# A two-layer graph network: one aggregate's products split a second time by Strassen in panel 3 of layer 0

## The chip, the cores and the metric

The kernel runs on one core of one Trainium2 chip. The time is the device time of one execution in microseconds (us); the number given for a kernel is the median of its runs. A profile records one further execution. In its views PE is the matmul engine, PEld its weight loads, DVE the vector engine, ACT the scalar engine, POOL the GpSimd engine and SP the engine that issues most DMAs; "L678" is line 678 of the kernel.

## What is computed

Two graph layers on 2708 nodes with 1024 features. Both normalise the rows, apply a relu, form attention scores between all nodes, mask them with the adjacency, take a softmax over the columns and multiply the attention by a projected matrix; the input is added back.

```python
h = jnp.maximum(_layernorm(x, axis=-1), 0.0)          # layer 0
f = h @ Wf + bf;  g = h @ Wg + bg
e = jax.nn.relu(f @ g.T)
attention = jax.nn.softmax(jnp.where(adj > 0, e, NEG), axis=1)
x = x + attention @ (h @ W + bW)

h = jnp.maximum(_layernorm(x, axis=-1), 0.0)          # layer 1
hw = h @ W1
e = jax.nn.leaky_relu(hw @ a1 + (hw @ a2).T, negative_slope=0.2)
attention = jax.nn.softmax(jnp.where(adj > 0, e, NEG), axis=1)
x = x + jax.nn.relu(attention @ hw)
```

Everything is fp32. The kernel uses that attention @ (h @ W) is (attention @ h) @ W: it first makes the *aggregate* attention @ h, then projects it.

## The kernel before

**Panels and pairs.** The 2708 rows are 20 tiles of 128 rows, one further tile and a rest of 20 rows (tiles 20 and 21, called MONO and TINY). The output rows are worked on in five panels of 576, 576, 532, 512 and 512 rows. The 20 full tiles form NQ = 10 pairs q = (2q, 2q+1), and two pairs form one of NK = 5 groups k.

**One level of Strassen.** Each large product is split once in Strassen's way (Winograd's form): seven products M1, M5, M2, M6, M3, M7, M4 in place of eight, with sums of the left and right operands in front of them and sums of the results behind. In the aggregate the left operand is h (split by halves of the features and by the even or odd tile of a pair), and the right operand is the transposed attention of a panel (split by the even or odd tile and by halves `lo`, `hi` of the panel's columns). A product of a 512-row panel is ten k-steps of four matmuls 128x128 by 128x256.

**Left operands in DRAM.** Layer 0's seven left operands lie in `hg_d[i]`, one DRAM tensor for each group i, with rows of W = 512 values. `rows_h` stores the four that are plain blocks of h (M1, M5's part, M2, M4), and `sums_h` makes the three sums in place. Layer 1's lie in `hr_d`, written by `pair_h`.

**The plain aggregate.** `aggregate(l, p, S, sm, then, rate)` (L923) makes the right sums on DVE (`second`, `fourth`) and calls `accumulate` (L664), which emits the matmuls of a product (L678) and after some k-steps and at the end of a product calls `behind(rate)`, four times a product. A left block for layer 0 is a load of 512 KB (`hc`, one group of one product), issued by `load` when its first matmul is emitted. `left_over` adds MONO and TINY to three results, `into_m15` to the fourth. PSUM results are evicted by DVE and ACT into `gT`; POOL scales them by the inverse row sums (L1020).

**The aggregate split twice.** `aggregate_quartered` (L1086) serves panels 1 to 4 of layer 1. Each of the seven products is split again: `product(m, n, ps, start)` (L1099) emits one of seven inner products, five groups k by two matmuls of (128x128 by 128x128 when the panel has 512 rows), L1113. The right inner sums are made on DVE by `make(m)` from `quarters_of` (L1033), 20 subtractions a product, into `quarter` tiles. The left inner sums of layer 1 are made earlier by `put_quarters(m, k)` (L405): a load of 512 KB in two halves issued by POOL into `hq`, four adds or subtractions of 256 columns on DVE, two stores of 256 KB by POOL into `hs2_d`. An inner product loads its left blocks (`hc2`, four groups, from `hr_d` or `hs2_d`), and a product loads the blocks of the fifth group once (`hl2`, two loads). `V` holds the product until it is added into its places.

**The order of the work.** For each panel p of layer 0: scores(p), project_q(p+1), aggregate(0, p), project(0, p). In front of the panel 4 aggregate stand scores(4) and project(0, 3). Two queues of small work are fed in between matmuls by a planner with prices in us: `later` (softmax pieces at 1.4, rows of the next layer, and so on) and `lazy` (the left sums of layer 1 at 1.7 each). `behind(us)` adds to a credit, and pops pieces while credit is left; `lazy` is served only when `later` is empty and `spare[0]` is set, which is so in layer 0's aggregates of panels 1 to 4. A piece's loads are issued ahead of it, when it is near the head of the list (`one`):

```python
def behind(us, psum_free=False):
    credit[0] = min(credit[0] + us, 2 * us)
    while later and credit[0] > 0 and ...:
        credit[0] -= one()
    while spare[0] and not later and lazy and credit[0] > 0:
        credit[0] -= one(lazy)
```

`softmax(p)` puts 24 pieces at the head of `later`. It is called after M2 of project_q, which from then on calls `behind(1.5)` 20 times; an aggregate calls `behind(3.0)` 28 times. Layer 1's seven left sums of a panel p enter `lazy` during scores(p+1), so that each of the aggregates of panels 1, 2 and 3 serves seven.

**What fixes an order.** `load` (L136) issues on SP and keeps program order. `store` (L140) issues on POOL, without it. `held(f)` keeps the vector instructions that f emits behind the vector instruction emitted before each; `by_gpsimd` (L1669) does the same for a DMA on POOL. Otherwise the scheduler at compile time may move an instruction. All stream tiles (`hc`, `hq`, `hc2`, `hl`, `hl2`, `adj_i`, `md`, ...) come from one pool of 12 tiles of 4 KB a partition; `slot` tiles come from a pool of 54.

Of the kernel before, what the change touches and what calls it, by code (L numbers as in the profile page):

```python
# [57 lines left out]
def kernel(  # L58
# [95 lines left out]
    groups = [[q, q + 1] for q in range(0, NQ, 2)]  # L154
    group_of = {q: (i, j) for i, g in enumerate(groups) for j, q in enumerate(g)}
    assert sorted(group_of) == list(range(NQ))
    hg_d = [dram.tile([P, 7, len(g), W], FP, name=f"hg_d{i}") for i, g in enumerate(groups)]
    NK = NQ // 2
    WH = W // 2
    hr_d = dram.tile([P, 7, 2, 2, NK, WH], FP, name="hr_d")  # L160
    hs2_d = dram.tile([P, 7, 4, NK, WH], FP, name="hs2_d")

# [41 lines left out]
    def one(of=None):  # L204
        of = later if of is None else of
        for it in of[:4 if of is lazy and from_slots[0] else ahead[0]]:
            if it[1]:
                it[1]()
                it[1] = None
        us, _, go = of.pop(0)[:3]  # L210
        go()
        return us
# [155 lines left out]
    def rows_h(q, ha, hb):  # L368

        i, j = group_of[q]  # L370
        for m, h in ((M1, ha[0]), (M5, ha[1]), (M2, hb[0]), (M4, hb[1])):
            store(hg_d[i][:, m, j], h)
# [3 lines left out]
    def sums_h():  # L376

        def fetch(q, two):
            i, j = group_of[q]
            for m in (M1, M2):  # L380
                two.append(stream("hr", (P, 2, W)))
                (load if "m" in got else by_scalar)(two[-1], hg_d[i][:, m:m + 2, j])

        def first(q, two):
            (a0, a1), (b0, b1) = ((t[:, 0], t[:, 1]) for t in two)
            add(b1, a1, b1)
            sub(a1, a0, a1)

        def second(q, two):
            (a0, a1), (b0, b1) = ((t[:, 0], t[:, 1]) for t in two)  # L390
            sub(a0, b1, a0)
            sub(b0, b0, a0)
            i, j = group_of[q]
            store(hg_d[i][:, M6:M7 + 1, j], two[0])
            store(hg_d[i][:, M3, j], b0)
            store(hg_d[i][:, M5, j], b1)
            summed[0] += 1
        for q in range(NQ):
            two = []
            put(1.4, lambda q=q, two=two: held(first, q, two), lambda q=q, two=two: fetch(q, two), ready=lambda: sums_may[0])  # L400
            put(1.4, lambda q=q, two=two: held(second, q, two), ready=lambda: sums_may[0])

    BY_QUARTERS = (M1, M5, M2, M6, M7, M3, M4)
    made_quarters = {}

    def put_quarters(m, k, to=lazy):
# [3 lines left out]
        def fetch():  # L410
            if from_slots[0]:
                two.extend(slot(f"hq{h}", (P, 2, WH)) for h in range(2))
            else:
                t = stream("hq", (P, 4, WH))
                two.extend(t[:, 2 * h:2 * h + 2] for h in range(2))
# [3 lines left out]
        def go():  # L419
# [5 lines left out]
            for h in range(2):  # L425
                store(hs2_d[:, m, 2 * h:2 * h + 2, k], two[h])
            made_quarters[m] = made_quarters.get(m, 0) + 1
        put(1.7, go, fetch, to=to)

    def quarters_until(m):  # L430
        while made_quarters.get(m, 0) < NK:
# [491 lines left out]
    def aggregate(l, p, S, sm, then={}, rate=3.0):  # L923
# [29 lines left out]
        steps = [(m, i) for m in order_of_products for i in range(len(groups))]  # L953

        def left(m, q, d):
            i, j = group_of[q]
            at = steps.index((m, i))
            for m_, i_ in steps[at:at + (3 if l else 1)]:
                if (m_, i_) not in hc:
                    hc[m_, i_] = stream("hc", (P, 4, WH) if l else (P, 2, W))  # L960
                    load(hc[m_, i_], hr_d[:, m_, :, :, i_].rearrange("p h f c -> p (h f) c") if l else hg_d[i_][:, m_])
# [71 lines left out]
    def quarters_of(p, S):  # L1033
# [50 lines left out]
        return {"make": make, "right": right, "first": first, "fifth": fifth, "second": second, "fourth": fourth}  # L1084

    def aggregate_quartered(p, S, sm, of_right, then={}, fine=1.2):  # L1086
# [12 lines left out]
        def product(m, n, ps, start):  # L1099
            quarters_until(m)  # L1100
            if (m, 0) not in lasts:
                for i, of in enumerate((hr_d[:, m, :, :, NK - 1].rearrange("p h f c -> p (h f) c"), hs2_d[:, m, :, NK - 1])):
                    lasts[m, i] = stream("hl2", (P, 4, WH))
                    load(lasts[m, i], of)
# [3 lines left out]
            load(t, hr_d[:, m, i // 2, i % 2, :NK - 1] if raw else hs2_d[:, m, i, :NK - 1])  # L1108
# [11 lines left out]
        def left_over(banks, e, s, fresh):  # L1120

            two = stream("hl", (P, W + 2 * P))
            load(two, hgl_d[1][:, e])
# [44 lines left out]
        def with_second():  # L1168
# [4 lines left out]
                       M7: lambda: make(M3), M3: lambda: make(M4)}  # L1173
        left_out = None
        for m in BY_QUARTERS:
            V = [quad(*direct[m])[:, 2 * r:2 * r + 2] for r in range(2)] if m in direct else [v[:, :, :h] for v in in_pairs("V")]
# [40 lines left out]
            if m == M5:  # L1217
                of_right["second"]()
            if m == M5:
                inverse.append(inverse_sums(p, sm))  # L1220
# [357 lines left out]
    def rows_done(t, xt):  # L1578
# [14 lines left out]
        if panel_of[t] == NP - 1:  # L1593
# [18 lines left out]
            else:  # L1612
# [16 lines left out]
                if q == NQ - 1:  # L1629
                    for m in BY_QUARTERS:  # L1630
                        put_quarters(m, q // 2, later)
# [17 lines left out]
        elif whole:  # L1649
# [3 lines left out]
            if quads_met[q // 2] == 2:  # L1653
                put(0.0, lambda: [put_quarters(m, q // 2) for m in BY_QUARTERS])
# [12 lines left out]
    ORDERED = (NP - 1,)  # L1667

# [98 lines left out]
    for p in range(NP):  # L1767
# [21 lines left out]
        G[p] = aggregate(0, p, S, got["sm"], then)  # L1789
        spare[0] = False  # L1790
        if p == 0:
            flush()
# [114 lines left out]
    for p in range(NP):  # L1907
# [6 lines left out]
        g = aggregate_quartered(p, S, sm, next_right, then, fine=1.0) if p else aggregate(1, p, S, sm, then, rate=4.0)  # L1914
# [34 lines left out]
```

## Time and profile before

| | us |
|---|---|
| median of 3 runs (lowest, highest) | 3050.46 (3048.57, 3051.97) |
| the profiled execution, its own time | 3055.39 |
| its span in the profile | 3053.6 |
| PE busy in the span | 2999.1 |
| DVE busy in the span | 2048.9 |
| layer 0, aggregate of panel 1 (from 839.95 to 988.06) | 148.11 |
| layer 0, aggregate of panel 2 (from 1236.95 to 1374.00) | 137.05 |
| layer 0, aggregate of panel 3 (from 1611.16 to 1743.16) | 132.00 |

All durations that follow come from the profiled execution; its span is 1.8 us shorter than its own time, and that time is 4.9 us above the median of the runs. In the profile's tables, "x" stands before a number of instructions. A wait is written "who <- whom it waited for: us in total, times, longest". Of the DMA, "share" is the mean busy share of the 16 DMA engines, and GB/s is what they moved. Times of instructions are counted from the start of the span.

### The profile page before, as it was taken

To read this page: it belongs to the slowest core of one execution; us is meant where nothing else is said; L and a number is where in the kernel's file an instruction comes from. 1 tells how busy PE (TensorE), PEld (TensorE's weight loads), DVE (VectorE), ACT (ScalarE), POOL (GpSimd) and SP (SyncE) were. 2 spreads that over 40 slices of the span, in tenths; PEclk is the share of its full clock that TensorE was granted. 3 is DMA by queue.
4 is the path that set the end of the run, shared out by engine and by line. 5 is a ranking of instruction groups with operands and counts; after the bars stand their busy time and mean duration, and the time that the engine had idled before them with its cause. 6 is when DMAs were issued, how large, how long until landed. Compare 5 with 4: busy or idle time off the path is not lost.

```text
span 3053.6 us, 41717 instructions
## 1 busy us (share of the span) xinstructions
PE 2999.1 (98%) x14642; PEld 2300.7 (75%) x14642; DVE 2048.9 (67%) x4667; ACT 536.5 (18%) x880; POOL 495.2 (16%) x770
## 2 busy tenths in 40 slices
PE   8998999999999999999999999999999999999999
PEld 4576777667877588885888886784767959879695
DVE  5776794585742686616965376867878768887863
ACT  3420020020200221101220111202232131212200
POOL 1421111210112110223101111131212010020201
PEclk9999999999999999999999999999999999999999
DMA  6989978887466785768957587678757768878797
GB/s 228 303 271 269 313 277 308 268 281 235 131 236 164 233 271 192 245 156 258 291 186 251 176 244 252 238 293 324 257 190 265 260 200 298 292 266 296 258 302 267
DMA packets 392704, 766.78 MB, mean 251 GB/s; under 512 B 65728, under 2 KB 206944, under 8 KB 392464
## 3 DMA queue, kind: packets, MB, share of 16 engines
q1 hardware_dynamic: 332336, 584.80, 59.4%
q0 software_dynamic: 54464, 164.78, 16.1%
q10 hardware_dynamic: 5696, 14.55, 1.4%
q8 instruction: 116, 1.90, 0.2%
q14 instruction: 92, 0.75, 0.1%
HBM read 630.04 MB, written 138.11 MB: 252 GB/s over the span
## 4 chain that ended last, share of the span: by engine, by line
PE 70%; issue 12%; DVE 11%; DMA 4%; POOL 2%; ACT 1%; SPq 0%; POOLq 0%; DVEq 0%; ACTq 0%
PE gy L678 6%; PE gz L678 6%; PE sz L1424 5%; PE gz L1113 5%; PE gx L678 5%; PE pz L1313 4%; PE px L1313 4%; PE sy L1424 3%; PE sx L1424 3%; PE gx L1113 3%; PE M_ps L591 3%; PE py L1313 3%; PE gy L1113 3%; PE gv L678 3%; DVE P L45 2%
## 5 line engine op out<-in xcount | busy, mean ns | idle before, releaser
L1424 PE MATMUL sz<-B,As 128*128 128x288 f32 (+2 forms) x1200 | 292.9, 393 | 5.4 <-DVE st L45 5.2
L1424 PEld LDWEIGHTS sz<-B,As 128*128 128x128 f32 x1200 | 228.3, 191 | 54.5 <-DVE st L45 8.4
L1424 PE MATMUL sx<-B,As 128*128 128x288 f32 (+2 forms) x800 | 201.3, 395 | 11.0 <-DMA As<-hs_d 9.3
L1424 PE MATMUL sy<-B,As 128*128 128x288 f32 (+2 forms) x800 | 199.0, 392 | 0.0
L1424 PEld LDWEIGHTS sx<-B,As 128*128 128x128 f32 x800 | 152.8, 192 | 44.0 <-DMA As<-hs_d 9.7
L678 PE MATMUL gz<-Sa,hc 128*128 128x288 f32 (+2 forms) x800 | 185.8, 393 | 0.0
L678 PEld LDWEIGHTS gz<-Sa,hc 128*128 128x128 f32 x800 | 151.7, 190 | 32.0 <-issue 2.2
L1424 PEld LDWEIGHTS sy<-B,As 128*128 128x128 f32 x800 | 152.0, 190 | 30.4 <-DVE st L45 0.3
L1113 PE MATMUL gz<-quarter,hc 128*128 128x128 f32 (+2 forms) x1344 | 168.9, 279 | 3.8 <-DVE gT L45 3.7
L1113 PEld LDWEIGHTS gz<-quarter,hc 128*128 128x128 f32 x1344 | 160.6, 191 | 5.1 <-DVE gT L45 4.6
L143 POOL DMA_DIRECT2D out_dram<-x_res x164 | 81.0, 500 | 469.1 <-DVE x_res L45 463.1
L1313 PE MATMUL py<-w,ps 128*128 128x512 f32 x320 | 142.1, 593 | 0.0
L1313 PE MATMUL pz<-w,ps 128*128 128x512 f32 x320 | 142.0, 595 | 0.0
L1313 PE MATMUL px<-w,gT 128*128 128x512 f32 x320 | 141.1, 593 | 0.0
L678 PE MATMUL gy<-T,hc 128*128 128x288 f32 (+2 forms) x480 | 115.0, 402 | 3.8 <-DMA hc<-hg_d 3.8
L1313 PEld LDWEIGHTS pz<-w,ps 128*128 128x128 f32 x320 | 60.3, 190 | 76.2 <-issue 72.1
L1313 PEld LDWEIGHTS py<-w,ps 128*128 128x128 f32 x320 | 60.6, 190 | 75.0 <-issue 72.6
L591 PE MATMUL M_ps<-wgT,wfT 128*128 128x512 f32 x256 | 112.7, 597 | 1.6 <-ACT hsT L45 1.6
L1313 PEld LDWEIGHTS px<-w,gT 128*128 128x128 f32 x320 | 60.2, 190 | 71.2 <-issue 67.8
L678 PEld LDWEIGHTS gy<-T,hc 128*128 128x128 f32 x480 | 93.2, 194 | 24.6 <-DMA hc<-hg_d 4.3
L143 POOL DMA_DIRECT2D mk_d<-mask x55 | 35.9, 652 | 455.6 <-DVE mask L45 427.3
L45 ACT ACTIVATE P<-P 128x576 f32<-128x576 f32 (+3 forms) x111 | 72.1, 650 | 207.3 <-DVE P L45 207.3
(391 smaller groups left out, 5829.0 us busy)
## 6 DMA issues: line engine op xcount, KB each, us to landing
hc<-hg_d SPq DMA_DIRECT2D x175, 512.0 KB
As<-hs_d SPq DMA_DIRECT2D x150, 512.0 KB
hc<-hr_d SPq DMA_DIRECT2D x119, 512.0 KB
hc<-hs_d SPq DMA_DIRECT2D x112, 512.0 KB
w<-wt_d SPq DMA_DIRECT2D x96, 512.0 KB
w<-in_L_gnn_W_dram SPq DMA_DIRECT2D x72, 512.0 KB
md<-md_d SPq DMA_DIRECT2D x56, 512.0 KB
adj_i<-in_adj_dram SPq DMA_DIRECT2D x200, 128.0 KB
```

Source lines behind the costliest of these rows:

```text
L45: i = f(*a, **k)
L143: nc.gpsimd.dma_start(a, b)
L591: nc.tensor.matmul(ps, wfT[a][c // NH][:, c % NH, :], wgT[b][c], start=(c == 0), stop=(c == NC - 1))
L678: nc.tensor.matmul(ps[d], left(m, k, d), right(m, k), start=(start and k == 0), stop=(k == K - 1), skip_group_check=True)
L1113: nc.tensor.matmul(ps[:, d], lhs[:, d * P:(d + 1) * P], inner_right(m, n, k), start=(start and k == 0 and d == 0), stop=(k == NK - 1), ski ...
L1313: nc.tensor.matmul(ps, left[i][m][:, k, :], w_[k], start=(start and k == 0), stop=(k == NH - 1), skip_group_check=True)
L1424: nc.tensor.matmul(ps[:n, :h], lefts[q][:, i % 2, c, :n], B[m][c // 2][:, c % 2, :h], start=(start and c == 0), stop=(c == NH - 1), skip_g ...
```

## The change

Layer 0's aggregate of panel 3 is made by `aggregate_quartered` too, with a new first argument l. In layer 0 its products M1 and M5 stay plain (through `accumulate`, rate 3.0), and M2, M6, M7, M3, M4 are split again, in this order; `behind` is called with 1.2 after each inner product. `V` takes a stream tile there. Their left inner sums are 25 new pieces of `lazy` (five products by five groups), put there after the aggregate of panel 0, at a price of 1.7. Each loads 512 KB from `hg_d` on SP in program order, does its four vector instructions held in order, and stores 2 x 256 KB by POOL in order into a second `hs2_d`. `lazy` now fetches for three pieces ahead instead of `ahead[0]`. `hg_d` becomes one tensor for all groups. An inner product of layer 0 that takes plain blocks loads them from `hg_d` in pieces of 1 KB.

```diff
-    hg_d = [dram.tile([P, 7, len(g), W], FP, name=f"hg_d{i}") for i, g in enumerate(groups)]
+    hg_d = dram.tile([P, 7, NK, 2, W], FP, name="hg_d")
-    hs2_d = dram.tile([P, 7, 4, NK, WH], FP, name="hs2_d")
+    hs2_d = [dram.tile([P, 7, 4, NK, WH], FP, name=f"hs2_d{l}") for l in range(2)]
...
     def one(of=None):
-        for it in of[:4 if of is lazy and from_slots[0] else ahead[0]]:
+        for it in of[:(4 if from_slots[0] else 3) if of is lazy else ahead[0]]:
...
-    BY_QUARTERS = (M1, M5, M2, M6, M7, M3, M4)
+    BY_QUARTERS = ((M2, M6, M7, M3, M4), (M1, M5, M2, M6, M7, M3, M4))
...
-    def put_quarters(m, k, to=lazy):
+    def put_quarters(l, m, k, to=lazy):
         def fetch():
+            if l == 0:
+                t = stream("hq", (P, 2, 2, WH))
+                load(t.rearrange("p f h c -> p f (h c)"), hg_d[:, m, k])
+                two.extend(t[:, :, h] for h in range(2))
+                return
...
             for h in range(2):
-                store(hs2_d[:, m, 2 * h:2 * h + 2, k], two[h])
-            made_quarters[m] = made_quarters.get(m, 0) + 1
-        put(1.7, go, fetch, to=to)
+                (by_gpsimd if l == 0 else store)(hs2_d[l][:, m, 2 * h:2 * h + 2, k], two[h])
+            made_quarters[l, m] = made_quarters.get((l, m), 0) + 1
+        put(1.7, (lambda: held(go)) if l == 0 else go, fetch, to=to)
...
-    def aggregate_quartered(p, S, sm, of_right, then={}, fine=1.2):
+    def aggregate_quartered(l, p, S, sm, of_right, then={}, fine=1.2, rate=3.0):
...
             if (m, 0) not in lasts:
-                for i, of in enumerate((hr_d[:, m, :, :, NK - 1].rearrange("p h f c -> p (h f) c"), hs2_d[:, m, :, NK - 1])):
+                rows = hr_d[:, m, :, :, NK - 1] if l else hg_d[:, m, NK - 1].rearrange("p f (h c) -> p h f c", h=2)
+                for i, of in enumerate((rows, hs2_d[l][:, m, :, NK - 1])):
                     lasts[m, i] = stream("hl2", (P, 4, WH))
-                    load(lasts[m, i], of)
+                    if l or i:
+                        load(lasts[m, i], of if i else of.rearrange("p h f c -> p (h f) c"))
+                    else:
+                        for h_ in range(2):
+                            load(lasts[m, i][:, 2 * h_:2 * h_ + 2], of[:, h_])
...
-            load(t, hr_d[:, m, i // 2, i % 2, :NK - 1] if raw else hs2_d[:, m, i, :NK - 1])
+            load(t, hs2_d[l][:, m, i, :NK - 1] if not raw else hr_d[:, m, i // 2, i % 2, :NK - 1] if l else
+                 hg_d[:, m, :NK - 1, i % 2, i // 2 * WH:(i // 2 + 1) * WH])
...
+        def collected():
+            if l == 0:
+                t = stream("V", (P, NH, h))
+                return [t[:, 2 * r:2 * r + 2, :h] for r in range(2)]
+            return [v[:, :, :h] for v in in_pairs("V")]
+
+        if l == 0:
...
+            exps_until(NQ)
+            of_right["fifth"]()
+            accumulate(left, of_right["operand"], NQ, h, (M1, M5), then,
+                       {M1: first_product, M5: lambda d, ps: add(quad(0, hi)[:, d], ps, quad(0, lo)[:, d])}, "g",
+                       {M5: sums_of_columns}, rate=rate, by_k=True, more={(M5, NQ // 2): with_second})
...
-        for m in BY_QUARTERS:
+        for m in BY_QUARTERS[l]:
...
+    SPLIT_EARLY = (3,)
...
-        G[p] = aggregate(0, p, S, got["sm"], then)
+        if p in SPLIT_EARLY:
+            G[p] = aggregate_quartered(0, p, S, got["sm"], quarters_of(p, S), then)
+        else:
+            G[p] = aggregate(0, p, S, got["sm"], then)
         spare[0] = False
         if p == 0:
+            for m in BY_QUARTERS[0]:
+                for k in range(NK):
+                    put_quarters(0, m, k)
             flush()
```

## The prediction

> **What bounds the kernel now.** I read the page first, then the busy time of each engine by stage, then the tensor engine's instructions in order of time, then waits, and last the DMA rate in stretches of 10 us around the panel 1 aggregate.
>
> The page's first part says that the matmul engine is the bound nearly everywhere:
>
> ```profile
> PE 2999.1 (98%) x14642; PEld 2300.7 (75%) x14642; DVE 2048.9 (67%) x4667; ACT 536.5 (18%) x880; POOL 495.2 (16%) x770
> ```
>
> By stage (stretch, its length, busy PE, weight loads, DVE, ACT, POOL, granted clock, DMA share, GB/s). The rows are layer 0's aggregates of panels 1, 2 and 3, then layer 1's of panels 3 and 4, which are already split twice:
>
> ```profile
> 839.95:988.06 148.11, 148.11 (x629) 114.35 (x629) 47.74 (x110) 6.04 (x13) 27.79 (x28) 1.00 0.66 200
> 1236.95:1374.00 137.05, 137.05 (x630) 114.34 (x629) 45.02 (x109) 4.60 (x11) 28.39 (x31) 1.00 0.69 208
> 1611.16:1743.16 132.00, 132.00 (x630) 114.35 (x629) 47.18 (x117) 11.13 (x16) 20.40 (x21) 1.00 0.71 223
> 2702.00:2830.00 128.00, 125.69 (x1132) 122.54 (x1131) 103.08 (x296) 23.06 (x44) 5.89 (x12) 1.00 0.87 301
> 2877.00:3000.00 123.00, 121.84 (x1115) 120.13 (x1114) 77.78 (x239) 8.71 (x20) 3.92 (x8) 1.00 0.90 304
> ```
>
> PE has no idle microsecond in the three aggregates of layer 0, so a microsecond that PE saves or waits there is one of the total. DVE has room (48 of 148). DMA is the second resource.
>
> The price of both forms of a product stands in PE's order of time (start, length, shape; two records are one matmul). Panel 3 as it is, then layer 1's panel 3:
>
> ```profile
> 1611.00 17.43 PE L678 MATMUL gx<-Sa,hc 128*128 128x256 f32 x80
> 1628.27 17.43 PE L678 MATMUL gy<-T,hc 128*128 128x256 f32 x80
> ...
> 2723.90 1.95 PE L1113 MATMUL gz<-quarter,hc 128*128 128x128 f32 x16
> 2725.68 0.61 PE L1113 MATMUL gz<-quarter,hl 128*128 128x128 f32 x4
> 2726.13 1.95 PE L1113 MATMUL gy<-quarter,hc 128*128 128x128 f32 x16
> ```
>
> A plain product takes 1628.27 - 1611.00 = 17.27 us (40 matmuls of 256 columns). An inner product takes 2726.13 - 2723.90 = 2.23 us (10 of 128), seven of them 15.63 us.
>
> **What the Trainium skill says.** "TensorE: Matmul & The Clock Gate", section "Back-to-back issue gap", gives N/2.4 + 2.5 ns for a matmul of N columns. The trace agrees up to a factor of four for this fp32 work: 17.27/40 = 432 ns is 4 x 108, 15.63/70 = 223 ns is 4 x 56. The saving is thus nearly the 1/8 of the columns, less the fixed part. "DMA: Bandwidth & Descriptors", section "Issuing engines are not separate DMA queues", says that DMAs started by SP, ACT and POOL run on the same 16 engines and interleave; its "Specifications" give a ceiling of 435 GB/s. Here the rate stops at 418 GB/s with share 1.03 (below), so moving a transfer to another queue makes no room. The first page's section "What's actually happening" says that an idle window of about 3.4 us halves the clock. The trace has that too, in layer 0's panel 0 aggregate, where DMA was full (chain in order of time: start, us):
>
> ```profile
> 506.16 7.68 DMA hc<-hg_d
> 513.88 7.18 PE gy L678 x16
> 521.07 19.40 PE gz L678 x80
> ```
>
> PE stood 7.7 us for its left blocks, then took 7.18 us for 16 records that take 19.40/5 = 3.88 warm: 3.3 us more.
>
> **Part 1: panel 3's matmuls.** Five products at 17.27 - 15.63 = 1.64 us less: -8.2. The left-over rows (tiles 20 and 21) cost four bursts, 2.46 us each in plain form (1659.35 to 1661.81) and 2.53 in the split form (2751.57 to 2754.10): +0.3. The order M1, M5, M2, M6, M7, M3, M4 swaps two products and costs nothing. Sum: **-7.9 us** of PE.
>
> **Part 2: panel 3's vector work.** Five times 20 subtractions for the right sums at 282 ns (row quarter<-P): 28 us. Evictions: 28 adds from PSUM at about 0.42 = 12, corner 2, 14 adds into place at 0.69 = 10, eight scalings at about 0.69 = 6, against some 24 evictions and one scaling that go (11). POOL loses three scalings of 5 us. DVE goes from 47 to about 47 + 28 + 30 - 11 = 94 of 124 us, less than the 103 of 128 in layer 1's panel 3. So it stays beside PE, apart from short waits. Layer 1's 28 products of this form show:
>
> ```profile
> PE gz L1128 <- DVE V L45: 4.5, 3, 2.2
> ...
> PE gz L1113 <- DVE gT L45: 3.7, 3, 1.4
> ```
>
> That is 8.2 us for 28 products; for five, **+1.5 us** (0 to 3). Behind those waits only the same product's next matmuls are queued.
>
> **Part 3: panel 3's loads.** Plain: 35 blocks of 512 KB. After: 10 plain and 5 x 9 = 55, +10.5 MB. 223 GB/s x 132 us = 29.4 MB become 39.9 in about 124 us, 322 GB/s, against 304 at share 0.90 in layer 1 with no wait on DMA. The V tiles and the masks' adj_i tiles also sit in the 12-tile stream pool. Unknown, 0 to +5 us; I take 0, because panel 3's seven layer 1 items fall in M1 and M5, which stay plain and leave DMA free (0.5 share after 1660), and keep 5 for the range. Putting hg_d in one tensor leaves rows of 4 KB as they are: 0 (a false dependence would fall on panel 0, whose sums are all issued before the products that read them).
>
> **Part 4: the left sums.** This decides. 25 items (five products, five k) join the lazy list after panel 0's aggregate, ahead of layer 1's. Each is one 512 KB load on SP, four subtractions or adds of 256 columns, two 256 KB stores on POOL:
>
> ```profile
> L45 DVE TENSOR_TENSOR hq<-hq x112: 404/406/427, 850.8 to 2198.4; 128x256 f32<-128x256 f32 x112
> L417 POOL DMA_DIRECT2D hq<-hr_d x70: 703/713/728, 810.7 to 2188.2; - x70
> L143 POOL DMA_DIRECT2D hs_d<-hq x70: 707/717/727, 852.2 to 2199.1; - x70
> ```
>
> DVE: 25 x 4 x 0.406 = 41 us, POOL: 50 x 0.717 = 36 us; both lie beside PE (DVE 48 of 148 busy). DMA is another matter, and first one must see *where* they fall. An aggregate calls behind(3.0) four times a product, 28 times: 84 us of credit. project_q has already paid for 23 of the 24 softmax pieces (first credit 3.0, then 19 calls of 1.5, at 1.4 each), so one is left, and lazy items start at once at 1.7 each. 1.4 + 25 x 1.7 = 43.9 is reached at the 15th call, inside the fourth product: **all 25 fall into panel 1's aggregate**, none into panel 2's. Layer 1's seven (panel 0's rows) follow up to the 19th call.
>
> SP's loads keep program order, so the left blocks (hc) of later products queue behind the items' loads; each needs one of 12 stream tiles, which an item gives back only when its stores have landed; and PE waits for hc. DVE's held items queue only before evictions that PE needs a product later; POOL's ordered stores sit before the residual's bias accumulations, not needed until 988. DMA around today's seven items:
>
> ```profile
> 860.00:870.00 10.00, 10.00 (x43) 7.86 (x42) 7.64 (x21) 0.00 (x0) 2.60 (x4) 1.00 1.02 400
> 870.00:880.00 10.00, 10.00 (x43) 7.85 (x42) 1.83 (x4) 0.00 (x0) 0.00 (x0) 1.00 1.03 418
> ```
>
> So DMA is full at about 409 GB/s, 1.28 us for 512 KB. The ledger to the 19th call, 4.75 products of 19.40 us after 840, at 932: 24 left blocks, 32 item loads, 30 items' stores (two still out) are 86 blocks. At most 12 (the tiles) are loaded before the first store is issued (852 today, DVE being full with softmax pieces until 850). 74 x 1.28 = 95 us of DMA against 932 - 853 = 79: **PE waits 16 us**. Bounds: if stores lag by the whole pool and DMA holds 418 GB/s, 64 x 1.25 = 80 against 79, +1; with 400 GB/s (97), 3 us of idle DMA between dependent steps and one loss of clock (3.3), +24. I take 16, the ledger with the shown rate. Panel 2's aggregate keeps its seven items: 0.
>
> **Sum.** -7.9 + 1.5 + 0 + 16 = +9.6 us. The profiled execution took 3055.39 us (span 3053.6), 4.9 above the median of the runs, 3050.46. The difference carries over: 3050.5 + 9.6 = **3060 us**. About 0.2% (6.1 us) is what a measurement can tell from no change.
>
> **The rivals.** *DMA hides the left sums* (on the not-slower side; the one mechanism is the lead that SP builds up). For it: today SP issues 14 left blocks by 866, whose last PE needs at about 890, and the seven items cost PE nothing; the aggregate as a whole has a DMA share of only 0.66. Against: 32 items follow each other at the rate of the seven. Price 1 us of waits: 3050.5 - 7.9 + 1.5 + 1 = 3045; waits up to 6 us keep it at 3050 or less. It turns slower where the waits pass 6.4 us.
>
> *Panel 3's loads bind too.* For: 322 GB/s wanted, stream tiles held by V and adj_i. Against: layer 1 at share 0.90 without a DMA wait. With the 16 us above and 5 here plus a loss of clock (3): 3068. If the left sums are hidden as in the first rival, 3045 + 5 = 3050.
>
> *The change does not do what it says:* items in both aggregates would need over 28 calls; the credits leave 9 calls unused, so I expect panel 2 without a layer 0 item. Were they spread evenly, each aggregate's ledger (12 or 13 items) would stay near its time, about 4 us of waits each: 3050.5 - 6.4 + 8 = 3052.
>
> **Chances.** Main case 0.54 (3054 to 3067). Left sums hidden 0.22 (3043 to 3050). Both bind 0.12 (3064 to 3076). Spread, or hidden with panel 3 bound, 0.12 (3046 to 3057). The range of 8 in 10 reaches from the hidden case's 3044 to 3070, leaving out the upper part of the third case and the ends. Faster by over 0.2% (under 3044.4) needs waits near zero: 0.18, most of the hidden case, since the price of each wait there is uncertain downwards too. Within 0.2%: 0.20. Slower: 0.62, the main case nearly whole and the third.
>
> **What would show it.** Part 1: inner products 2.23 us apart in panel 3, its aggregate near 132 - 7.9 + 1.5 = 126 us. Part 2: waits of gz for V and gT of about 1 us, DVE near 94. Part 3: no wait of PE for hc2 or hl2. Part 4: in panel 1's aggregate DMA share near 1 at about 400 GB/s from 850 to about 940, PE waiting for hc, and a length of 148 + 16 = 164 us; all of the layer 0 items there. I am wrong if that aggregate stays under 154 us, or if panel 3's is longer than 132.

## The result, and the profile after

The changed kernel took **3071.14 us** (median of 4 runs, 3070.28 to 3072.07), the kernel before 3050.57 in the same session: a ratio of 1.0068 with a 95% interval of 1.0055 to 1.0080, some 21 us slower. The prediction was 3060. The profiled execution has a span of 3068.5 us, against 3053.6; that is only 14.9 us more, since a profiled execution is one among the runs of its kernel: before's lies 4.9 us above their median, after's 0.9 below, and two of the experiments' (e2, e5) 8 below.

The profile's busy times, in the form in which the prediction shows them of before:

```profile
PE 2998.7 (98%) x15006; PEld 2304.9 (75%) x15006; DVE 2119.6 (69%) x4896; ACT 539.9 (18%) x890; POOL 525.1 (17%) x818
```

PE's busy time has hardly moved (2999.1 before): the split took matmul time away in panel 3, and something gave it back elsewhere. By stage (stretch, its length, busy PE, weight loads, DVE, ACT, POOL, granted clock, DMA share, GB/s), layer 0's aggregates of panels 1, 2 and 3:

```profile
837.92:1011.11 173.19, 157.59 (x630) 118.22 (x628) 83.45 (x210) 6.05 (x13) 71.91 (x90) 0.95 0.92 321
1259.98:1397.02 137.04, 137.04 (x629) 114.15 (x629) 45.20 (x109) 4.79 (x11) 28.09 (x32) 1.00 0.69 208
1634.23:1760.17 125.94, 124.42 (x994) 118.99 (x992) 82.90 (x246) 9.51 (x22) 12.99 (x19) 1.00 0.93 301
```

Panel 3's aggregate went from 132.00 to 125.94 us, panel 2's did not change, and **panel 1's went from 148.11 to 173.19, 25.1 us more**. In panel 1's row two different losses can be read: 173.19 - 157.59 = 15.6 us in which PE did nothing, and 157.59 - 148.11 = 9.5 us by which the same 630 records took longer, at a mean granted clock of 0.95. The difference of these two stages, 25.1 - 6.1 = 19.0 us, is nearly the whole of the measured loss. The other stages together are 4.1 us shorter in this pair of profiles; they differ as much between kernels that are alike there (layer 0's scores of panel 0 lie between 162.3 and 167.2 us in the profiles of this study).

PE's order of time in panel 1's aggregate (start, length, instructions, in brackets the idle time before it and its releaser; a line is a burst, a run of matmuls without a break; at the full clock 16 records are 4.12 us, 8 are 2.10):

```profile
868.43 5.81 PE L678 MATMUL gy<-T,hc 128*128 128x288 f32 x16 [3.19 <-DVE hq L45]
874.92 4.12 PE L678 MATMUL gy<-T,hc 128*128 128x288 f32 x16 [0.69 <-DMA hc<-hg_d]
881.67 5.81 PE L678 MATMUL gy<-T,hc 128*128 128x288 f32 x16 [2.63 <-DVE hq L45]
...
906.26 3.90 PE L970 MATMUL gx<-Sa,hl 128*128 128x288 f32 x8 [3.03 <-DMA hl<-hgl_d]
...
939.97 8.03 PE L678 MATMUL gy<-Sb,hc 128*128 128x288 f32 x32 [1.76 <-DMA hc<-hg_d]
952.31 6.80 PE L678 MATMUL gy<-Sb,hc 128*128 128x288 f32 x16 [4.31 <-DMA hc<-hg_d]
```

Six waits, 15.6 us together, all for left blocks (where DVE's hq is named, I read it as a left block too: no matmul here reads hq, and the right operand T had been made by 848.4). Four of the bursts behind them run slow: 1.7 + 1.7 + 1.8 + 2.7 = 7.9 of the 9.5 us. Most of the rest is the start of a burst itself: 16 records on their own take 4.12 us, and 19.56 / 5 = 3.91 within a run of 80. The DMA in stretches of 10 us has share 1 there, as it had in two stretches before:

```profile
870.00:880.00 10.00, 8.35 (x29) 5.76 (x27) 0.20 (x1) 0.00 (x0) 1.05 (x2) 0.88 1.02 415
880.00:890.00 10.00, 8.33 (x28) 6.29 (x29) 9.96 (x30) 0.00 (x0) 4.27 (x6) 0.83 1.03 418
910.00:920.00 10.00, 10.00 (x47) 7.59 (x47) 1.25 (x3) 1.60 (x4) 4.20 (x6) 1.00 1.03 417
```

In panel 3, PE's order of time shows the inner products 2.24 us apart (1674.10 - 1671.86), and the stage's waits are two short ones:

```profile
1671.86 1.95 PE L1119 MATMUL gz<-quarter,hc 128*128 128x128 f32 x16
1673.65 0.61 PE L1119 MATMUL gz<-quarter,hl 128*128 128x128 f32 x4
1674.10 1.95 PE L1119 MATMUL gy<-quarter,hc 128*128 128x128 f32 x16
```

```profile
PE gz L1119 <- DMA hc<-hg_d: 0.9, 1, 0.9
PE gx L1119 <- DMA hc<-hg_d: 0.6, 1, 0.6
```

### The profile page after: what moved, and what is told of

The parts are those of the page before. It is cut to its first block, busy times and chain, and to the rows that moved or that the text cites. A ratio compares the mean times of both kernels' runs of the same rounds, so it can differ in the third digit from the quotient of the medians.

```text
span 3068.5 us, 42894 instructions
## 1 busy us (share of the span) xinstructions
PE 2998.7 (98%) x15006; PEld 2304.9 (75%) x15006; DVE 2119.6 (69%) x4896; ACT 539.9 (18%) x890; POOL 525.1 (17%) x818
## 4 chain that ended last, share of the span: by engine, by line
PE 68%; DVE 13%; issue 9%; DMA 7%; POOL 2%; ACT 1%; SPq 1%; POOLq 0%; DVEq 0%; ACTq 0%
PE sz L1457 6%; PE gz L1119 6%; PE gy L678 5%; PE sx L1457 4%; PE gz L678 4%; PE sy L1457 4%; PE gx L1119 4%; PE gy L1119 4%; PE pz L1346 4%; PE px L1346 4%; PE py L1346 3%; PE M_ps L591 3%; PE gx L678 3%; DVE P L45 2%; PE qz L678 2%
## 5 line engine op out<-in xcount | busy, mean ns | idle before, releaser
L1119 PE MATMUL gz<-quarter,hc 128*128 128x128 f32 (+2 forms) x1584 | 198.3, 278 | 4.7 <-DVE gT L45 3.7
L1119 PEld LDWEIGHTS gz<-quarter,hc 128*128 128x128 f32 x1584 | 188.6, 191 | 6.3 <-DVE gT L45 4.6
L678 PE MATMUL gz<-Sa,hc 128*128 128x288 f32 (+2 forms) x640 | 150.6, 395 | 0.0
L678 PEld LDWEIGHTS gz<-Sa,hc 128*128 128x128 f32 x640 | 121.2, 190 | 27.8 <-issue 1.8
L45 DVE TENSOR_TENSOR hq<-hq 128x256 f32<-128x256 f32 x212 | 79.4, 414 | 52.5 <-DMA hq<-hr_d 36.4
```

The costliest lines, as they stand in the source:

```text
L45: i = f(*a, **k)
L678: nc.tensor.matmul(ps[d], left(m, k, d), right(m, k), start=(start and k == 0), stop=(k == K - 1), skip_group_check=True)
L1119: nc.tensor.matmul(ps[:, d], lhs[:, d * P:(d + 1) * P], inner_right(m, n, k), start=(start and k == 0 and d == 0), stop=(k == NK - 1), ski ...
```

## The experiments

All are edits of the changed kernel and are timed against the kernel before; the length of panel 1's aggregate is abbreviated A1 (148.11 us before, 173.19 after). The theory was the prediction's: the DMA cannot carry 25 items and the left blocks in that time, and the stream tiles come back late. The rivals were that the order of issue on SP alone makes left blocks late, and that each item costs something wherever it stands. A lone A1 rests on one profiled execution. The two kernels with the same 25 items in the same place and no remedy, the changed one and e1, have 173.19 and 171.58: a difference of 2 us in A1 says nothing, and one of 5 us is weak by itself.

### Only the left sums, without the split

```diff
-    SPLIT_EARLY = (3,)
+    SPLIT_EARLY = ()
```

> The 25 left sums are made and then not used: panel 3's aggregate of layer 0 is plain again. Theory (the loss is all in panel 1's aggregate, from the left sums; the split itself gains 6 us): panel 1's aggregate 173 us as in the changed kernel, panel 3's 132, total 3050.6 + 25 = about 3076, slower than the changed kernel by 6. Rival (the split itself costs elsewhere, for example in the scores of panel 4 behind it or in layer 1's delayed sums): total below 3071.

Measured: 3076.47 us, ratio 1.0075 (1.0056 to 1.0093). A1 171.58, panel 3's aggregate 132.00. The loss comes from the sums alone. The split as such is worth 6 us by the length of its stage; the ratios with and without it (1.0068 and 1.0075) are too close to show it. A1's row:

```profile
841.91:1013.49 171.58, 153.62 (x629) 115.76 (x628) 83.68 (x210) 6.05 (x13) 71.76 (x90) 0.98 0.93 325
```

Here PE stood 171.58 - 153.62 = 18.0 us and lost 153.62 - 148.11 = 5.5 to slower matmuls, against 15.6 and 9.5 in the changed kernel. The sum of both is nearly the same (23.5 and 25.1), how it divides is not.

### Which resource makes the left blocks late: SP's order, the tiles

Items loaded by POOL in place of SP, so that no item's load stands in SP's order:

```diff
-                load(t.rearrange("p f h c -> p f (h c)"), hg_d[:, m, k])
+                nc.gpsimd.dma_start(t.rearrange("p f h c -> p f (h c)"), hg_d[:, m, k])
```

> The 25 loads are issued by POOL as layer 1's are, and not by SP: same bytes, same tiles, but no left block stands behind an item's load on SP. Theory A (DMA is full): panel 1's aggregate stays within 4 us of 173 and the total near 3070. Theory B (order on SP: left blocks stand behind loads that wait for a tile): the waits of PE for hc fall to a few us, aggregate near 155, total near 3053.

Measured: 3074.43, ratio 1.0066 (1.0044 to 1.0088), A1 175.27. No gain: PE still stands 14.0 us for left blocks (and 5.9 for an eviction, see below), so standing behind the items' loads on SP is not what costs. This agrees with the Trainium skill, "DMA: Bandwidth & Descriptors", section "Issuing engines are not separate DMA queues": another issuer makes no room.

Two more stream tiles (and three slots fewer, to make room):

```diff
-    slots = ctx.enter_context(tc.tile_pool(name="slots", bufs=54))
-    strm = ctx.enter_context(tc.tile_pool(name="strm", bufs=12))
+    slots = ctx.enter_context(tc.tile_pool(name="slots", bufs=51))
+    strm = ctx.enter_context(tc.tile_pool(name="strm", bufs=14))
```

> The stream pool has 14 tiles and not 12 (the slot pool 51 and not 54, to make room). Theory A (DMA is full): two more blocks can be loaded ahead, 2 x 1.28 = 2.6 us less, panel 1's aggregate about 170, total about 3068. Theory B (too few tiles: SP waits for a tile that an item holds): a sixth more tiles takes away a third of the waits or more, aggregate 160 to 165, total 3058 to 3063. Fewer slots may cost something elsewhere, which the other stages show.

Measured: 3071.27, ratio 1.0049 (1.0031 to 1.0067), A1 164.33. A1 is 8.9 us less, so tiles seem to count; but by the whole kernel the gain is not clear, since the interval overlaps that of the changed kernel (1.0055 to 1.0080). The next edit is clearer.

Layer 0's results written to slots and stored from there, so that an item's stream tile is free after its fourth vector instruction, and not when its stores have landed:

```diff
+            if l == 0:
+                new = [slot(f"hn{h}", (P, 2, WH)) for h in range(2)]
+                o11, o12, o21, o22 = (new[h][:, i] for h in range(2) for i in range(2))
+                add(o22, a21, a22)
+                sub(o21, a11, a21)
+                sub(o11, o22, a11)
+                sub(o12, a12, o11)
+                for h in range(2):
+                    by_gpsimd(hs2_d[l][:, m, 2 * h:2 * h + 2, k], new[h])
```

> Layer 0's left sums are written into tiles of the slot pool and stored from there, so that the stream tile is free after the fourth vector instruction, not when the stores have landed. Bytes, order and density are those of the changed kernel. Theory A (DMA is full): panel 1's aggregate within 3 us of 173. Theory B (tiles held until the stores land keep SP from issuing left blocks): panel 1's aggregate 148 to 158, total 3047 to 3056.

Measured: 3064.65, ratio 1.0031 (1.0019 to 1.0043), A1 162.99. The largest of SP's own waits in this stage, for a tile whose stores have to land first, becomes less than half (of after, then of e7, where all that is left is of layer 1's items):

```profile
SPq L139 <- DMA hs_d<-hq: 87.4, 27, 10.7
SPq L139 <- DMA hs_d<-hq: 40.1, 10, 15.1
```

So about 10 of the 25 us go with the tiles. The other 15 stay.

### Fewer items in the time: a higher price, and where the rest then goes

```diff
-        put(1.7, (lambda: held(go)) if l == 0 else go, fetch, to=to)
+        put(1.7 if l else 5.0, (lambda: held(go)) if l == 0 else go, fetch, to=to)
```

> A left sum of layer 0 costs 5.0 of credit and not 1.7, so that some 17 fall into panel 1's aggregate and 8 into panel 2's. Theory (rate: it is the 7 items a product that overfill DMA or the tile pool): 2.4 items a product, 2.4 x 1.05 + 2.6 = 5.1 MB in 19.4 us = 265 GB/s; no waits, aggregates 148, 137 and 126 us, total about 3044.5, faster than before by 0.2%. Rival (number: each item costs PE about 1 us wherever it lies, by the tile that it holds and the order on SP): aggregates of panels 1 and 2 together still some 25 us longer than before, total about 3070.

Measured: 3080.62, ratio 1.0089 (1.0068 to 1.0110), where a gain was expected. A1 is 148.11, without one wait: thinned out, 17 items in this aggregate cost nothing. But the stage after it, project of panel 1, went from 61.80 to 75.73 and panel 2's aggregate from 137.04 to 150.56. PE's waits, from 800 to 1400:

```profile
PE py L1346 <- DMA w<-wt_d: 9.9, 1, 9.9
PE sum_ps L902 <- DVE gT L45: 9.2, 1, 9.2
```

The loss moved. An item fetched at the end of the aggregate stands, with its tile and its loads, in front of the weights that the next stage needs at once: SP stood 7.0 us for the stores of items while it had to load weights. And in panel 2's aggregate, with 8 items of layer 0 and 14 of layer 1, DVE stood for loads of layer 1 (3.5 and 2.2 us, the last two) in front of an eviction that PE needed. The profiled execution took 3072.56; what the median has above it, 8 us, is in no trace.

A milder price, 2.4, for layer 0's items and layer 1's of group 0:

```diff
+        put(2.4 if l == 0 or k < 1 else 1.7, (lambda: held(go)) if l == 0 else go, fetch, to=to)
```

> All 32 items stay in panel 1's aggregate but at a price of 2.4, five a product over the whole aggregate instead of seven over the first two thirds. DMA wanted: 5 x 1.05 + 2.6 = 7.9 MB in 19.4 us, 405 GB/s, its full rate. Theory A (DMA is full at 410): waits of a few us, aggregate 150 to 156. Theory B (tiles): five items a product hold 5/7 of the tiles; waits shrink but stay, aggregate 155 to 165.

Measured: 3068.97, ratio 1.0050 (1.0034 to 1.0065), A1 167.29, project 64.98: longer than either theory gave, and already a little into the next stage. Density is only half of it. Of 14.6 us of waits 7.2 are for left blocks; 7.4 are for an eviction, in front of which DVE stands for layer 1's loads (9.3, 1.8, 1.6 and 1.3 us):

```profile
948.64 1.80 DVE L45 TENSOR_TENSOR hq<-hq 128x256 f32<-128x256 f32 x4 [9.26 <-DMA hq<-hr_d]
959.97 2.49 PE L902 MATMUL sum_ps<-sm,ones 128*128 128x288 f32 x4 [7.42 <-DVE gT L45]
```

Price 4.0 for layer 0's items and layer 1's of groups 0 and 1, with what has been fetched worked off before the stage ends:

```diff
+        put(4.0 if l == 0 or k < 2 else 1.7, (lambda: held(go)) if l == 0 else go, fetch, to=to)
...
+        while p in (1, 2) and lazy and lazy[0][1] is None:
+            one(lazy)
```

> All left sums in front of panel 3 (layer 0's 25 and layer 1's first 14) cost 4.0 of credit, three a product instead of seven, and whatever is already fetched at the end of an aggregate is finished there, so that no item holds a tile in the projection behind. Theory (density: too many items a product, by tiles and by DMA): aggregates of panels 1 and 2 at 148 and 137 us, the projection between them 61.8, panel 3's aggregate 125.5, total 3050.6 - 6 = about 3045, faster than before by some 0.2%. Rival (each item costs wherever it lies): total still above 3060.

Measured: 3089.31, ratio 1.0119 (1.0102 to 1.0135); A1 152.39, project 99.76. The edit was faulty: `one` fetches ahead each time it is called, so the loop never met an item that was not fetched and emptied the whole list at the end of panel 1's aggregate. All its loads then stood before the weights of project:

```profile
PE py L1346 <- DMA w<-wt_d: 20.5, 1, 20.5
PE px L1346 <- DMA w<-in_L_gnn_W_dram: 15.7, 2, 11.6
```

It says nothing for or against spreading, but much about the place: project took 99.76 - 61.80 = 38 us more with the items that were left. The same with panel 4's aggregate split as well (`SPLIT_EARLY = (3, 4)`):

> As e6_spread, and panel 4's aggregate of layer 0 is split again too, with the same left sums in DRAM. If the split gains the same there, its aggregate falls from 130.5 to about 125 and the total to about 3039. Against: the rows of panel 3 and 37 pieces of small work share that aggregate, and V takes stream tiles.

Measured: 3107.43, ratio 1.0176 (1.0161 to 1.0191), with the same fault (project 99.57). Panel 4's aggregate gained 2.2 us (130.5 to 128.3), and layer 1's first aggregate lost 16 to 20 (155.6 in the kernel before, 151.2 in e6, 171.5 here).

### What remains when tiles come back early: bytes, and the order of layer 1's pieces

e7 with half of each item's load: the left half of the columns, used for both halves. The kernel leaves out the other half of the operand; matmuls, vector work and stores are as many as before.

```diff
-                load(t.rearrange("p f h c -> p f (h c)"), hg_d[:, m, k])
-                two.extend(t[:, :, h] for h in range(2))
+                load(t[:, :, 0], hg_d[:, m, k, :, :WH])
+                two.extend(t[:, :, 0] for h in range(2))
```

> Results in slots as in e7_results_in_slots, in the changed kernel's own places (all 25 in panel 1's aggregate), and each item loads only the left half of its columns and uses it for both halves (so layer 0's panel 3 is computed from wrong sums; the work of the engines and the stores is unchanged). 25 x 0.25 MB fewer, 6.5 MB, 16 us at 410 GB/s. If the 14.9 us that e7_results_in_slots still loses are bytes above what the DMA moves: panel 1's aggregate 148 to 151. If they are the vector engine's or the queue's order: 160 or more, as there.

Measured: 3058.86, ratio 1.0021 (1.0014 to 1.0029), A1 160.03. Outside what the byte theory gave. But for 30 us from 861 the DMA was still full, with 1.55 times as many packets for fewer bytes (of e12, then of e7), since these halves are rows of 1 KB:

```profile
DMA packets 5536, 11.81 MB, mean 394 GB/s; under 512 B 615, under 2 KB 3337, under 8 KB 5534
DMA packets 3569, 12.40 MB, mean 413 GB/s; under 512 B 546, under 2 KB 546, under 8 KB 3567
```

So the cut was made in whole rows instead:

```diff
+                load(t[:, 0].rearrange("p h c -> p (h c)"), hg_d[:, m, k, 0])
+                two.extend(t[:, 0] for h in range(2))
```

> As e12_slots_half_loads, with the half cut the other way: each item loads the left block of one of its two tiles in whole rows of 2 KB and uses it for both (layer 0's panel 3 is computed from wrong sums). The same 6.5 MB fewer, without the packets of 1 KB, of which e12 had 1.5 times as many in the burst. If the smaller packets took back what the bytes gave: panel 1's aggregate 150 to 155. If bytes are only a small part of what remained in e7_results_in_slots: 158 or more, as in e12.

Measured: 3060.70, ratio 1.0020 (1.0008 to 1.0033), A1 160.61. By its length alone this says "bytes are only a small part". PE's order of time says otherwise: the burst of items from 861 to 911 has **no wait at all** (in e7 there are seven before 916, 9.8 us), and one wait follows. PE, then DVE, of this kernel:

```profile
902.32 15.68 PE L689 MATMUL gz<-Sa,hc 128*128 128x288 f32 x64
927.32 6.87 PE L689 MATMUL gz<-Sa,hc 128*128 128x288 f32 x16 [9.31 <-DMA hc<-hg_d]
```

```profile
912.83 1.81 DVE L45 TENSOR_TENSOR hq<-hq 128x256 f32<-128x256 f32 x4 [13.38 <-DMA hq<-hr_d]
```

SP issues nothing between 897.6 and 919.8, with the DMA at share 0.55 from 911 to 921. DVE stands 13.4 us for a load of layer 1 (hr_d); five loaded items of layer 0 are behind it in DVE's order (their sums, hn<-hq, follow at 919.6), and hold their tiles. Layer 1's pieces are not held, so the scheduler has put them in front of the last layer 0 pieces, on DVE and on POOL. This was a third cause, in no theory so far, though the waits for an eviction in e2, e3 and e8 (9.2, 5.9 and 7.4 us) have the same root: in each, DVE stands for layer 1's loads just before it. Holding layer 1's pieces of this aggregate tests it, here and in the changed kernel itself and in e7:

```diff
-                (by_gpsimd if l == 0 else store)(hs2_d[l][:, m, 2 * h:2 * h + 2, k], two[h])
+                (by_gpsimd if l == 0 or k < 1 else store)(hs2_d[l][:, m, 2 * h:2 * h + 2, k], two[h])
...
-        put(1.7, (lambda: held(go)) if l == 0 else go, fetch, to=to)
+        put(1.7, (lambda: held(go)) if l == 0 or k < 1 else go, fetch, to=to)
```

> The changed kernel with layer 1's seven pieces of panel 1's aggregate (group 0) held in order too, their vector instructions and their stores, so that none of them can stand in front of the last layer 0 pieces on DVE or POOL. Order theory (the two waits at 940 and 952, 6.1 us, and the slow matmuls after them, some 4 us, come from DVE standing for a layer 1 load while loaded layer 0 tiles behind it keep the stream pool full): panel 1's aggregate 162 to 164, its waits before 910 unchanged. Theory that DMA and tiles alone make the waits: 170 or more.

Measured: 3065.03, ratio 1.0036 (1.0023 to 1.0049), A1 168.26: 4.9 us less, half of what the order theory gave (by the ratio of the whole kernel some 10 us less). Of the two late waits, 6.1 us, one of 1.1 us is left, but the four early ones grew from 9.5 to 11.7 us: one limit is lifted and another binds more.

> e13_slots_half_rows with the same order for layer 1's pieces (again from wrong sums in layer 0's panel 3). In e13 the burst from 861 to 911 ran without a wait, and one wait of 9.3 us followed while SP issued nothing for 22 us. Order theory: that wait goes, panel 1's aggregate 148 to 150. If it stays at 156 or more, the order isn't what made it.

Measured: 3052.96, ratio 0.9994 (0.9985 to 1.0003), A1 151.62. The 9.3 us wait is gone, and the longest is now 1.1 us; A1 is 1.6 us above what the order theory allowed.

> e7_results_in_slots with the same order for layer 1's pieces: whole bytes, tiles given back early. Order theory: the wait of 1.4 us at 933 goes, those before 916 (9.8 us) stay, since they come from the bytes: panel 1's aggregate 158 to 162. If it falls to 152 or less, bytes were not what remained; if it stays at 163 or more, the order plays no part here.

Measured: 3064.23, ratio 1.0038 (1.0024 to 1.0053), A1 163.88: with e7's tiles and whole loads the order brings nothing that can be seen, and the waits before 916 stay. The rows of panel 1's aggregate, of e14, e16 and e15 in turn:

```profile
840.60:1008.90 168.30, 155.49 (x630) 117.27 (x629) 85.56 (x210) 6.06 (x13) 71.73 (x90) 0.96 0.93 332
```

```profile
842.60:1006.50 163.90, 151.59 (x630) 114.58 (x629) 84.59 (x210) 5.96 (x13) 71.67 (x90) 0.99 0.95 341
```

```profile
843.90:995.52 151.62, 149.36 (x629) 113.82 (x628) 84.71 (x210) 6.05 (x13) 71.80 (x90) 1.00 0.95 334
```

Read as a chain, each step one edit (idle is length less PE busy; slower is PE busy less 148.11):

| kernel | A1 | PE idle | slower matmuls |
|---|---|---|---|
| after | 173.2 | 15.6 | 9.5 |
| + layer 1's pieces in order (e14) | 168.3 | 12.8 | 7.4 |
| + tiles free before the stores land (e16) | 163.9 | 12.3 | 3.5 |
| + 6.5 MB fewer loaded (e15) | 151.6 | 2.3 | 1.3 |

The last step is the largest, 12.3 us, of the 16 us that 6.5 MB take at 410 GB/s: most of what is left once tiles and order are mended goes with the bytes. (Half a load also fills its tile sooner, which these runs do not separate from the bytes.) The first two steps cannot be split: in A1 order alone gave 4.9, tiles alone 10.2 (e7), both together 9.3, and by the ratios of the whole kernel order (1.0036), tiles (1.0031) and both (1.0038) are alike, some 10 us under the changed kernel's 1.0068. Either mend does it, and the second adds nothing that can be seen. e15 (0.9994) stands clear of all three.

### The items thinned out evenly, none begun near the end

Price 3.0 for layer 0's items and layer 1's of groups 0 and 1, the latter held too (as above, with `k < 2`), and in front of the two last products of panels 1's and 2's aggregates the fetched pieces are finished and no further one is begun until the next aggregate:

```diff
+    def no_more():
+        while lazy and lazy[0][1] is None:
+            lazy.pop(0)[2]()
+        spare[0] = False
...
+        put(3.0 if l == 0 or k < 2 else 1.7, (lambda: held(go)) if l == 0 or k < 2 else go, fetch, to=to)
...
+        if p in (1, 2):
+            then[M3] = no_more
```

> The left sums thinned out: layer 0's 25 blocks and layer 1's blocks that are made before panel 2's aggregate ends are put at a price of 3.0 (about 20 of them in the first five products of an aggregate instead of 25 in three), and in the two last products of panels 1's and 2's aggregates none is begun. The matmuls are those of the changed kernel. Density theory (25 us are lost because 8 items in a product's 19.4 us ask for more than the DMA moves, and because their tiles come back late): 3.9 items a product are about (3.9 x 1.05 + 2.62) MB in 19.4 us, some 345 GB/s against 410 that the engines gave: panel 1's aggregate 148, what follows it 61.8, panel 2's aggregate 137, panel 3's 125.5, the whole about 6 below the kernel before, some 3045. Theory that the sums cost whatever their place, because each block takes a tile of the stream and a store that returns late: panel 1's aggregate 155 or more, the whole at or above the kernel before.

Measured: **3047.23 us** against 3052.06, ratio 0.9977 (0.9968 to 0.9986) (13 and 50 runs): by that interval 4 to 10 us faster than the kernel before. The rows of panel 1's aggregate, the project after it, and the aggregates of panels 2 and 3:

```profile
840.80:988.91 148.11, 148.11 (x629) 114.31 (x629) 75.99 (x170) 6.05 (x13) 45.12 (x53) 1.00 0.87 295
988.91:1050.71 61.80, 61.80 (x145) 27.39 (x144) 36.69 (x87) 10.45 (x15) 12.08 (x19) 1.00 0.88 266
1237.80:1374.84 137.04, 137.04 (x629) 114.30 (x629) 60.14 (x149) 4.80 (x11) 59.55 (x74) 1.00 0.86 285
1612.30:1737.68 125.38, 124.37 (x994) 119.03 (x993) 83.05 (x246) 9.54 (x22) 12.93 (x19) 1.00 0.94 303
```

PE is busy for every microsecond of the first three. 22 of the 25 items of layer 0 are loaded for panel 1's aggregate, three for panel 2's. Layer 1's seven have moved too: none is left in panel 1's aggregate, and panel 2's has all 14. So the stage has 22 items where the changed kernel has 32, and it has them at a lower rate. After the first six loads, 16 follow in e9 between 848.8 and 925.3; in the changed kernel, after the first eight, 17 between 853.6 and 913.0. An item moves 1.05 MB (its load and its stores), a product's five left blocks 2.62 MB in 19.4 us, 135 GB/s. Worked out for a PE that does not wait: 16 x 1.05 / 76.5 us + 135 = 355 GB/s, against 17 x 1.05 / 59.4 us + 135 = 436. What the DMA moved in these stretches (e9, then after, where PE did wait):

```profile
848.80:925.30 76.50, 76.50 (x321) 59.54 (x320) 43.73 (x115) 3.19 (x8) 22.15 (x32) 1.00 0.91 337
853.60:913.00 59.40, 49.87 (x185) 36.23 (x185) 35.87 (x99) 2.00 (x5) 27.06 (x38) 0.91 0.99 375
```

In the stretches of 10 us read here it gave at most 419 (877.92 to 887.92 in the changed kernel). That layer 1's seven are gone is not enough by itself: in e14, where they stay but in order, only one wait of 1.1 us falls among them, and 11.7 us of waits come ahead of them. The edit changes density, order and end at once. Density alone (e2) frees panel 1's aggregate and loses in the two stages behind; which of the other two mends those was not tested apart.

The same with results in slots (e7's edit):

> As e9_even, with layer 0's results written to slots and stored from there, so that the stream's tile is free after its fourth sum. Density theory: tiles do not bind at 3.9 items a product, so the same as e9_even within 1.5 us. Tile theory: panel 1's aggregate shorter than e9_even's by 3 or more.

Measured: 3047.51, ratio 0.9983 (0.9976 to 0.9990), A1 148.11. The same as e9. SP's waits for stores, 62.6 us in e9's panel 1 aggregate, are gone, and PE, which had no wait there, gains nothing: at this density the tiles do not bind. The theory that a block costs wherever it stands is out with e9.

## Why the prediction was wrong, step by step

**Part 1 (-7.9): right.** Panel 3's aggregate was to be 126 us and was 125.94; inner products 2.24 us apart, PE busy 124.42 us.

**Part 2 (+1.5): right in size by luck.** PE waited 1.5 us there, but for left blocks; the waits for DVE that the term stood for did not come. DVE was busy 82.9 us, 11 less than the sum of Part 2 (94), which cost nothing as it lay beside PE.

**Part 3 (0): 1.5 us too low.** 301 GB/s, share 0.93, for the 322 worked out; the two short waits on hc are its whole cost, and make up for those of Part 2.

**Part 4 (+16): the step that failed, in size.** Place and mechanism were as written: all 25 items in panel 1's aggregate, none in panel 2's, the DMA full at 415 to 418 GB/s, PE waiting for hc. The measured term is 25.1 us, above even its upper bound of 24. "PE waits 16 us" was met (15.6). Missing are the 9.5 us of slower matmuls: the text had seen that PE lost clock after a wait of 7.7 us, and put "one loss of clock (3.3)" into the upper bound, but the value taken had none. With it the sum is 3050.5 + 9.6 + 9.5 = 3069.6, against 3071.14. A term that says PE waits 16 us needs the price of the restarts in its centre; here it added 9.5 us to 15.6 of waiting, and in e1 5.5 to 18.0.

That the 16 itself was met is partly luck. The 16 was a ledger of bytes. With tiles and order mended (e16), the idle time is 12.3 us, and 10 of these go when 6.5 MB do (e15): the bytes look worth some 12, not 16. What made up for it is tiles held until their stores land, named in the text but priced only as a bound, and layer 1's pieces in front of the last layer 0 ones, which it did not see: "Layer 1's seven (panel 0's rows) follow up to the 19th call" takes the list's order for the engines' order, which only holds for held instructions.

**The rivals.** *DMA hides the left sums* is refuted for this density and true at e9's: its 3045 against 3050.5, a ratio of 0.9982, lies inside e9's interval. *Panel 3's loads bind too* is out (125.94). *Spread over both aggregates* did not happen; what it was to cost, some 4 us of waits in each, was too much for panel 1's aggregate, where 17 (e2) or 22 (e9) items cost PE nothing, and too little for e2's panel 2 aggregate, which lost 13.5.

Open stays how the first 9 us divide between tiles and order, why e1 has more waiting and less slow time than the changed kernel, and why one wait of 3 us costs clock and another does not (below).

## What to carry to other kernels

In these runs background transfers were free where their rate plus the foreground's stayed under what the DMA gave in that very stretch (355 GB/s worked out, against at most 419), and cost where it did not (436). So let a planner's price come from the time of an item's bytes beside the foreground, not from its vector work (here 1.7 and 2.4 were too dense and 3.0 was free). Stop them some way before a stage's end, because what is fetched last stands in front of the next stage's first loads. Where an engine takes its instructions in order, a small piece that waits for a load stands in front of all that follows, so fix the order of such pieces. Where PE is the bound and is made to wait, count the restarts at the lower clock into the forecast, and where an experiment's length says "no effect", look whether the wait has moved before believing it.

## What the runs showed of the hardware

The Trainium skill, "TensorE: Matmul & The Clock Gate", section "What's actually happening", has the clock go to half after an idle window of about 3.4 us. The traces show slow bursts behind shorter waits too: 2.63 us (16 records in 5.81 us, warm 4.12) and 3.19 us (5.81) in the changed kernel, 2.18 us (5.78) in e12. Others of the same length were free: 2.97 us (4.15) in e16, 3.00 us (4.12) in e7, 3.11 us (4.12) in e1. Of e12, e16 and e1:

```profile
926.26 5.78 PE L689 MATMUL gz<-Sa,hc 128*128 128x288 f32 x16 [2.18 <-DMA hc<-hg_d]
902.83 4.15 PE L689 MATMUL gx<-Sb,hc 128*128 128x288 f32 x16 [2.97 <-DMA hc<-hg_d]
885.20 4.12 PE L678 MATMUL gy<-T,hc 128*128 128x288 f32 x16 [3.11 <-DVE hq L45]
```

So between 2.2 and 3.2 us either happened. In panel 1's aggregates of eight kernels (after, e1, e7, e12 to e16) no wait of 2.1 us or less was followed by a slow burst, and each of more than 3.3 us was.

The same skill's "DMA: Bandwidth & Descriptors", section "Queues, rings and completion order", says that each DMA engine serves the queues in turn. In e7's burst of items (861.7 to 891.7, 413 GB/s; packets, MB, share of the 16 engines' time) SP's queue, which has the left blocks and the items' loads, had 56%, and POOL's 46%:

```profile
q1 hardware_dynamic: 1875, 6.85, 56.4%
q0 software_dynamic: 1692, 5.53, 45.8%
```

Stores whose data nobody reads until panel 3 took nearly half of the engines' time while PE stood waiting for left blocks.
